# A two-layer graph network with top-p attention: fewer candidates in the second search, and one statistics step a slot later

## The chip, the cores and the metric

The kernel runs on one core of one Trainium2 chip. The metric is the time of one execution on the device in microseconds (us), lower is better; a kernel's time is the median of several runs. The core has five engines that work side by side[...]: TensorE (PE in the profile; its weight loads are shown apart as PEld), VectorE (DVE), ScalarE (ACT), GpSimd (POOL) and SyncE (SP), which only issues DMAs. Each engine carries out its own instructions in the order in which the program issues them.

## The reference

x is a table of 2708 nodes with 256 features, adj a sparse 2708 x 2708 adjacency (about 8 nonzeros a row and the diagonal). Layer 0 is

```
s = adj @ x
x = layernorm(x + relu(concat(x, s) @ weight + bias))
```

Layer 1 makes two steps on two streams, one over the row-normalised adjacency R (with the identity added), one over an attention A that is computed anew in each step:

```
for n in 0, 1:
    A  = top_p_attention(Xa)     # 2708 x 2708
    Xf = R @ Xf
    Xa = A @ Xa
    Z += Xf @ U1[n].T + Xa @ U2[n].T
h = layernorm(X + Z) * ln_g + ln_b
out = layernorm(x + h)
```

The attention takes the softmax of a bilinear form of the rows, keeps in each row the largest probabilities until those ahead of one sum to 0.9 (an element stays while the sum before it is under 0.9), sets the rest to zero and normalises the row again. Ties are cut in order of columns. So each row needs its own threshold.

## The kernel before, in words

**Blocks.** The 2708 rows are 22 blocks of 128 (the last, the edge, has 20). A block of attention is a tile `e` of 128 rows by 2708 (padded to 2720) columns. The kernel first does layer 0 (to about 290 us), then step 1 of layer 1 over the 22 blocks (to about 745 us), then step 2, where the change lies. The order of all instructions is written out by hand; nothing is planned by a scheduler.

**The fast path and the general path.** All of this is `fast_path`. It takes shortcuts in the search that need not hold for every input, and collects flags that tell whether they did. At the end the flags are summed, and if one is set, `general_path` computes layer 1 again with a plain search.

**The search of step 2.** Per block, ScalarE computes the exponentials and their sum z while it reads the logits (`exps2`, L844), and estimates from them a first level l0 (threshold z/l0). Two tries on ScalarE (`try_act`, L966 and L969: a Relu pass and a Sign pass over the block each) find the mass above a level; from it `next_level` makes the next level with the constants `STEPS`. `last_level` on VectorE picks the start: the last level if the count and mass rule with `FEW` accepts it, else the one before, else nothing. Then, all on VectorE:

- `below_level` (L1023): one pass over the block that keeps the elements below the start level in `low` and adds them up. It reads two tensors.
- `candidates` (L1030): the 8 largest of each of NS2 segments of SEG2 elements, by MAX8.
- `in_order` (L1039, L1042): the TOP2 largest of the candidates in order, by MAX8 and MATCH_REPLACE8 in turn, eight at a time.
- `threshold` (L1058 to L1078): a running sum over these, the element at which the mass reaches 0.9, and how many elements equal to it are kept in each of 4 windows of the row.
- `mark` (L1083), four times: writes the kept ties of one window into `w`.
- `mask` (L1088): one pass over the block that sets all below the threshold to zero and sums the rest. It reads two tensors too.

Afterwards TensorE transposes the masked block (`turn`, L527), ScalarE copies the transposes out (L530), and TensorE multiplies them with the values (`products`, L564).

**The loop of step 2.** One pass `per` of the loop works on four blocks at once: exponentials of block `per`+2, tries of block `per`+1, start level and candidates of block `per`, order, threshold, marks and mask of block `per`-1, product of block `per`-2. A pass has six slots g, one for each group of four transposes. In each slot TensorE's work is issued first, then ScalarE's, then one part of VectorE's (`next(vector)`, a generator in `vector_slots`), then what `later` holds, then `final_slot(g)`. The parts of VectorE are: slot 0 the first seven steps of the order in turn with the last-level arithmetic; 1 the below pass; 2 the rest of the order in turn with eight candidate segments, two at a time; 3 the threshold's steps in turn with the remaining segments, two at a time; 4 marks 0 and 1; 5 mark 2, the sum of z (L852, for block `per`+2), mark 3, two small operations, and the mask.

**The other stream.** Step 2's loop also carries both products with R. R is sparse, so each block m has a list of at most 896 columns, and `y_load` gathers the rows of the other operand: seven indirect DMAs (L719) of 128 rows of 1 KB, issued on GpSimd. Two buffers `yg` take turns; `r_load` issues block m+1's when block m starts. TensorE's units of it (`r_units`, L749, eight to a block) are spread over the slots: 144 over passes 2 to 9 for the first product, 176 over passes 11 to 21 for the second, which is 16 units or two blocks a pass.

**The end of a block.** When a block's two sums have met (`arrive`, L792), it is `ready`. `final_slot` brings it through two layernorms: slot 2 takes up to two ready blocks as `new`; slot 3 computes statistics of `new` and of `finals`, the blocks of the pass before (L1182, L1183: the first and the second layernorm); slot 5 the roots on ScalarE (L1218, L1219); slot 0 of the next pass one small product on VectorE (L1222), then for `finals` the last normalisation and for `new` the middle: a normalisation on ScalarE (L1192) into a `spares` tile and a multiplication and an addition on GpSimd (L1207, L1208), after which `new` become `finals`. These four GpSimd operations a pass stand in one queue with the gathers. Slot 1 stores what is done.

Of the kernel before, what the change touches and what calls it, by code (L numbers as in the profile page):

```python
# [21 lines left out]
CH = 512  # L22
SEG = 170
NS = 16
SEG2 = 136
NS2 = 20
TOP1 = 64
TOP2 = 48
WS = 4

GUESS = 2.76141059
STEPS = ((0.93339875, 14.44678062, 82.55022771), (0.98700001, 8.00991560, 128.06811957))
FEW = 20.0
TOP_S = 0.8999
TIE_EPS = 1.5e-5
KS = 7
# [14 lines left out]
def gnn_two_layer_kernel(ctx: ExitStack, tc: tile.TileContext, N, xT_d, x_d, adj_d, w0_d, b0_d,  # L53
# [29 lines left out]
    assert N % 2 == 0 and NB % 2 == 0 and N * 2.0 ** -15 < 0.09 and DC == 2 and DA == 64  # L83
    assert SEG * (NS - 1) + 8 <= N <= SEG * NS == SEG2 * NS2 and N >= SEG2 * (NS2 - 1) + 8
    assert NB == 3 * KS + 1 and CW == P and CAP % 8 == 0 and N < NB * P
# [63 lines left out]
def fast_path(ctx, tc, c, flags, fint, xT_d, x_d, w0_d, b0_d, w1_d, w2_d, w3_d, u1_d, u2_d, g_d, b_d):  # L149
# [297 lines left out]
    for m in range(NB):  # L447
# [35 lines left out]
        if m >= ML:  # L483
            i = m - ML
# [82 lines left out]
    def seg_max(dst, src, p, step, width):  # L567
        for i in range(NS):
            w = min(width, N - SEG * i) if step == SEG else width
            nc.vector.max(dst[:p, i * 8:(i + 1) * 8], src[:p, i * step:i * step + w])  # L570

    def put_in_order(dst, n, cand, p):

        spare = small.tile([P, NS2 * 8], FP, tag="spare", name="spare", bufs=1)[:, :cand.shape[1]]
        src = cand
# [11 lines left out]
    def extract1(t):  # L587
        p = rows(t)
        e = es[t % 4]
        cand = small.tile([P, NS2 * 8], FP, tag="cand", name="cand", bufs=2)[:, :NS * 8]  # L590
        seg_max(cand, e, p, SEG, SEG)
# [385 lines left out]
    def next_level(b, k):  # L977
        keep, slope, down = STEPS[k]
        nc.scalar.activation(b.kept, b.l[k], AF.Copy, scale=keep + TOP_P * slope, bias=-down)
        nc.scalar.activation((b.l1, b.l2)[k], b.u[k], AF.Identity, bias=b.kept, scale=-slope)  # L980
        if k:
            nc.scalar.activation(b.few, b.l1, AF.Copy, scale=TOP_P, bias=-FEW)

# [5 lines left out]
    def try_dve(b, k):  # L989
# [5 lines left out]
        if k == 0:  # L995
            keep, slope, down = STEPS[0]
            nc.vector.tensor_scalar(b.kept, b.l0, keep + TOP_P * slope, -down, op0=ALU.mult, op1=ALU.add)
# [20 lines left out]
    def below_level(b):  # L1018
# [5 lines left out]
                                       accum_out=bulk[:p, 2, t:t + 1])  # L1024
        b.cand = small.tile([P, NS2 * 8], FP, tag="cand", name="cand", bufs=2)

    def candidates(b):
        p = b.p
        for i in range(NS2):
            nc.vector.max(b.cand[:p, 8 * i:8 * i + 8], low[:p, SEG2 * i:SEG2 * (i + 1)])  # L1030
            yield

    def in_order(b):
        p = b.p
        b.srt = small.tile([P, TOP1 + 1], FP, tag="srt", name="srt", bufs=3)
        spare = small.tile([P, NS2 * 8], FP, tag="spare", name="spare", bufs=1)
        src = b.cand
        for i in range(0, TOP2, 8):
            nc.vector.max(b.srt[:p, i:i + 8], src[:p])  # L1039
            yield  # L1040
            if i + 8 < TOP2:
                nc.vector.match_replace(spare[:p], b.srt[:p, i:i + 8], src[:p], -3.0e38)  # L1042
# [3 lines left out]
    def threshold(b):  # L1046


        t, p = b.t, b.p
        s = b.srt[:p, :TOP2]  # L1050
        sc = small.tile([P, 3 + 2 * WS], FP, tag="sc", name="sc", bufs=3)
# [4 lines left out]
        x = sums  # L1056
        q_ = small.tile([P, TOP1], FP, tag="qs", name="qs", bufs=1)[:p, :TOP2]
        nc.vector.scalar_tensor_tensor(need, b.z, TOP_P - 1.0, below, op0=ALU.mult, op1=ALU.add)  # L1058
        nc.vector.tensor_tensor_scan(x[:p, 1:TOP2 + 1], s, s, 0.0, op0=ALU.add, op1=ALU.bypass)
        yield  # L1060
        nc.vector.scalar_tensor_tensor(q_, x[:p, 1:TOP2 + 1], need, s, op0=ALU.is_ge, op1=ALU.mult)
        yield
# [97 lines left out]
    new, finals, done = [], [], []  # L1160
# [56 lines left out]
    def roots(a, b):  # L1217
        nc.scalar.activation(sds[:, a:b], mvs[:, a:b, 1], AF.Ln, bias=c.eps, scale=1.0)  # L1218
        nc.scalar.activation(sds[:, a:b], sds[:, a:b], AF.Exp, scale=-0.5)  # L1219

    def over(a, b):
        nc.vector.scalar_tensor_tensor(nbs[:, a:b], mvs[:, a:b, 0], -1.0, sds[:, a:b], op0=ALU.mult, op1=ALU.mult)  # L1222

    def final_slot(i):


        if i == 2:
            while ready and len(new) < 2:
                new.append(Final(*ready.pop(0)))
                new[-1].load()  # L1230
        if i == 1:
            while done:
                done.pop().store()
        n = len(new) + len(finals)
        if i == 3:
            for k, f in enumerate(new + finals):
                f.stats(k)
        if i == 5 and n:
            roots(0, n)
        if i == 0 and n:  # L1240
            over(0, n)
            for f in finals:
                f.end()
            for f in new:
                f.middle()
            done[:] = finals
            finals[:] = new
            new.clear()
# [23 lines left out]
    for per in range(NB + 2):  # L1272
# [11 lines left out]
        for g in range(NG):  # L1284
# [30 lines left out]
            if g == 0:  # L1315
                final_slot(0)
                if t_mul:
                    t = t_mul - 1
                    base = za_load(t)
                    later[1].append(lambda t=t, base=base: arrive(t, base, accs.pop(t), ras.pop(t)[:rows(t)]))  # L1320
            for f in now:
                f()
            if g and (per < NB + 1 or g < NG - 1):
                final_slot(g)
# [407 lines left out]
```

## Time and profile before

| | us |
|---|---|
| median of 3 runs | 1303.6 (1302.28 to 1304.17) |
| the profiled execution, its own time | 1308.28 |
| its span (first to last instruction) | 1306.5 |
| PE busy | 1236.7 (95%) |
| DVE busy | 997.3 (76%) |
| ACT busy | 735.6 (56%) |
| POOL busy | 641.9 (49%) |

The profile is one execution, taken by the hardware profiler. Its page gives busy times by engine, the chain of work that ended last, and groups of instructions: line, engine, operation, what it writes and reads, how often, busy time and the mean duration of one, idle time of the engine before it and what ended that. The trace behind it answers for any stretch of time. A group's busy time counts overlapping instructions once, so busy over count is less than the mean duration. Times of a timeline are us from the span's start. A busy PE isn't PE at its peak, and an engine's gaps between instructions aren't counted as busy even where the engine could not have been faster.

The loop of step 2 runs from about 757 to 1290 us. The masks (L1088) start at 779.33, 810.42, 832.75, 856.54 and so on to 1282.64; from one to the next it takes between 20.7 and 25.2 us from the second on, and 15.5 us to the last.

### The profile page before, as it was taken

Reading aid. Unit: us, or ns where it says so; the run is one execution under the profiler, and the core shown is the slowest. Engines: PE = TensorE matmul, PEld = TensorE weight load, DVE = VectorE, ACT = ScalarE, POOL = GpSimd, SP = SyncE. Lnnn points to the kernel's source line nnn. Section 1 sums busy time; section 2 is a strip of 40 time slices with the busy share of each in tenths; the row PEclk is TensorE's granted clock in tenths of the full one; section 3 lists DMA queues with packets and bytes.
Section 4 is the critical chain, followed back from the end, with each engine's and each line's share of the span. In section 5 each row is a group of like instructions: output and inputs, shape, how many; then the busy total and the mean of one; then the engine's idle time right before and its main releaser. Section 6 shows DMA issues by size and latency. Waiting matters only on the chain.

```text
span 1306.5 us, 18895 instructions
## 1 busy us (share of the span) xinstructions
PE 1236.7 (95%) x5764; PEld 892.9 (68%) x5764; DVE 997.3 (76%) x3406; ACT 735.6 (56%) x1337; POOL 641.9 (49%) x594
## 2 busy tenths in 40 slices
PE   7999999979899999999999978999999999999975
PEld 5878778843477777777777556777765777766753
DVE  2455445884999997977771279989888999999996
ACT  1010110125456656655665488887888989989821
POOL 1000000002465442577666068878775778888850
PEclk9999999999999999999999888999999999999898
DMA  7455445423322220132324145565663645555551
GB/s 189 152 171 165 149 160 169 148 89 105 119 81 84 70 71 12 40 93 92 91 85 107 49 150 156 177 184 169 185 145 114 197 143 161 175 169 156 151 121 38
DMA packets 101704, 166.00 MB, mean 127 GB/s; under 512 B 17362, under 2 KB 74070, under 8 KB 101594
## 3 DMA queue, kind: packets, MB, share of 16 engines
q1 hardware_dynamic: 75308, 108.65, 26.0%
q0 software_dynamic: 20544, 51.17, 15.1%
q10 hardware_dynamic: 5742, 4.89, 1.4%
q8 instruction: 48, 0.79, 0.3%
q14 instruction: 62, 0.51, 0.1%
HBM read 130.74 MB, written 33.90 MB: 126 GB/s over the span
## 4 chain that ended last, share of the span: by engine, by line
PE 77%; DVE 10%; ACT 6%; DMA 3%; POOL 2%; issue 1%; SPq 0%; ACTq 0%; POOLq 0%; DVEq 0%
PE acc L564 26%; PE acc L257 16%; PE lg L507 9%; PE misc L749 9%; PE tr L527 7%; PE acc L651 2%; DVE e L1088 2%; DVE w L1083 2%; PE acc L462 2%; PE misc L426 2%; PE acc L672 2%; PE misc L699 2%; DMA xT<-in_xT 1%; POOL yg L719 1%; ACT e L844 1%
## 5 line engine op out<-in xcount | busy, mean ns | idle before, releaser
L530 ACT COPY wT<-tr 128x512 f32<-128x512 f32 (+2 forms) x258 | 132.0, 519 | 216.8 <-PE tr L527 215.8
L564 PE MATMUL acc<-x,wT 128*128 128x256 f32 (+1 forms) x924 | 230.5, 388 | 0.0
L564 PE MATMUL acc<-ya,wT 128*128 128x256 f32 (+1 forms) x924 | 228.1, 386 | 0.0
L719 POOL DMA_INDIRECT yg<-v_d,ix x154 | 196.6, 1277 | 59.8 <-issue 23.2
L719 POOL DMA_INDIRECT yg<-yf_d,ix x154 | 191.6, 1244 | 48.3 <-issue 23.1
L564 PEld LDWEIGHTS acc<-x,wT 128*128 128x128 f32 (+1 forms) x924 | 165.2, 189 | 71.0 <-issue 37.4
L257 PE MATMUL acc<-y,adj_t 128*128 128x257 f32 (+1 forms) x924 | 208.4, 381 | 0.0
L564 PEld LDWEIGHTS acc<-ya,wT 128*128 128x128 f32 (+1 forms) x924 | 170.6, 191 | 44.5 <-issue 24.0
L749 PE MATMUL misc<-yg,adj_t 128*128 128x256 f32 (+1 forms) x704 | 185.1, 396 | 14.0 <-DMA yg<-v_d,ix 6.6
L257 PEld LDWEIGHTS acc<-y,adj_t 128*128 128x128 f32 (+1 forms) x924 | 171.8, 189 | 32.7 <-issue 8.9
L367 POOL DMA_INDIRECT adj_t<-in_adj,ix x154 | 167.8, 1089 | 51.8 <-issue 44.1
L749 PEld LDWEIGHTS misc<-yg,adj_t 128*128 128x128 f32 (+1 forms) x704 | 124.2, 191 | 67.2 <-issue 21.5
L507 PE MATMUL lg<-k,q 64*128 64x512 f32 (+3 forms) x528 | 150.2, 596 | 14.0 <-ACT e L848 7.0
L527 PE MATMUL tr<-ident,e 128*128 128x128 f32 (+2 forms) x946 | 148.5, 276 | 7.5 <-DVE e L1088 6.3
L527 PEld LDWEIGHTS tr<-ident,e 128*128 128x128 f32 (+2 forms) x946 | 113.0, 140 | 52.1 <-issue 24.0
L334 POOL DMA_DIRECT2D part_d<-e x1 | 0.6, 573 | 290.3 <-DVE e L333 290.3
L966 ACT ACTIVATE e<-e,st 128x2708 f32<-128x2708 f32 (+1 forms) x43 | 113.5, 2640 | 0.1
L439 ACT COPY x1T<-tr 128x256 f32<-128x256 f32 (+1 forms) x22 | 8.0, 364 | 186.6 <-PE tr L438 186.6
L969 ACT ACTIVATE e<-e,st 128x2708 f32<-128x2708 f32 (+1 forms) x42 | 110.9, 2641 | 0.1
L570 DVE MAX8 cand<-e 128x8 f32<-128x170 f32 (+1 forms) x352 | 87.2, 317 | 26.6 <-ACT e L514 26.6
L1030 DVE MAX8 cand<-w 128x8 f32<-128x136 f32 (+1 forms) x440 | 105.9, 284 | 0.0
L1083 DVE MATCH_REPLACE8 w<-part,e 128x680 f32<-128x680 f32 (+1 forms) x88 | 74.3, 850 | 0.0
(238 smaller groups left out, 1732.3 us busy)
## 6 DMA issues: line engine op xcount, KB each, us to landing
adj_t<-in_adj SPq DMA_DIRECT2D x44, 704.0 KB
adj_t<-adjc_d SPq DMA_DIRECT2D x44, 448.0 KB
adjc_d<-adj_t SPq DMA_DIRECT2D x22, 256.0 KB
base<-za_d SPq DMA_DIRECT2D x40, 128.0 KB
adjc_d<-adj_t SPq DMA_DIRECT2D x22, 192.0 KB
xt<-in_x ACTq DMA_DIRECT2D x21, 128.0 KB
x_d<-x SPq DMA_DIRECT2D x21, 128.0 KB
x1b_d<-xb SPq DMA_DIRECT2D x21, 128.0 KB
```

The costliest lines, as they stand in the source:

```text
L257: nc.tensor.matmul(acc[:p, :n], lhsT=halves[k // KH][:kw, k % KH, :p], rhs=y[:kw, k, :n], start=k == 0, stop=stop and k == NB - 1)
L367: nc.gpsimd.indirect_dma_start(out=a[:CW, i, :], out_offset=None, in_=adj_rows, in_offset=bass.IndirectOffsetOnAxis(ap=ix[:CW, m, i:i + 1] ...
L507: nc.tensor.matmul(lg[:p, h, :b - a], lhsT=q[o, t * P:t * P + p], rhs=keys[s][o, i, :b - a], start=True, stop=True)
L527: nc.tensor.transpose(tr[:kw, k % 4, :p], e[:p, k * P:k * P + kw], ident[:p, :p])
L530: nc.scalar.copy(wT[:, :full, :p], tr[:, :full, :p])
L564: nc.tensor.matmul(acc[:p, :D], lhsT=wT[:kw, k % 4, :p], rhs=y[:kw, k, :], start=k == 0, stop=k == NB - 1)
L719: nc.gpsimd.indirect_dma_start(out=y[:CW, i, :], out_offset=None, in_=rows_d, in_offset=bass.IndirectOffsetOnAxis(ap=ix[:CW, m, i:i + 1], ...
L749: nc.tensor.matmul(acc[:p, :D], lhsT=a[:kw, k, :p], rhs=y[:kw, k, :], start=k == 0, stop=k == CC)
L966: nc.scalar.activation(scr[:b.p, :N], e, AF.Relu, bias=b.nz, scale=b.l[k], accum_out=b.relu)
L969: nc.scalar.activation(scr[:b.p, :N], e, AF.Sign, bias=b.nz, scale=b.l[k], accum_out=b.sign)
L1030: nc.vector.max(b.cand[:p, 8 * i:8 * i + 8], low[:p, SEG2 * i:SEG2 * (i + 1)])
L1083: nc.vector.match_replace(w[:b.p, W * i:W * (i + 1)], b.part[:b.p, i, :], e2(b.t)[:b.p, W * i:W * (i + 1)], 3.0e38)
```

## The change

Three things, all in step 2:

- The candidates come from 16 segments of 170 elements instead of 20 of 136: 16 MAX8 a block over 170 elements, and 128 candidates instead of 160. The four tie windows stay 680 elements wide, four segments each instead of five.
- 40 of the candidates are put in order instead of 48: five MAX8 and four MATCH_REPLACE8 over 128 elements instead of six and five over 160. The order stream has nine steps instead of eleven, so two are left for slot 2 instead of four; slot 3 is left with eight segments instead of twelve. The constants of the levels are others.
- In `final_slot`, the second statistics (of `finals`) are issued in slot 4, behind marks 0 and 1, instead of slot 3, behind the threshold. Those of `new` stay in slot 3.

```diff
-SEG2 = 136
-NS2 = 20
+SEG2 = 170
+NS2 = 16
 TOP1 = 64
-TOP2 = 48
+TOP2 = 40
 ...
-STEPS = ((0.93339875, 14.44678062, 82.55022771), (0.98700001, 8.00991560, 128.06811957))
-FEW = 20.0
+STEPS = ((0.97048, 13.37709, 72.87486), (1.01755, 9.09506, 145.60103))
+FEW = 17.8171
 ...
         if i == 3:
-            for k, f in enumerate(new + finals):
+            for k, f in enumerate(new):
                 f.stats(k)
+        if i == 4:
+            for k, f in enumerate(finals):
+                f.stats(len(new) + k)
         if i == 5 and n:
             roots(0, n)
```

## The prediction

> **What bounds the kernel now.** The page puts PE at 95% busy and at 77% of the chain that ended last, and DVE at 76%. But the change cuts DVE work in step 2 alone, so the shares over the span say little; I cut the span at the starts of the mask pass (L1088) and took the busy time of each engine in three such stretches (one pass each over a block):
>
> ```profile
> core 0: us, PE busy (x) PEld busy (x) DVE busy (x) ACT busy (x) POOL busy (x), PEclk, DMA share, GB/s
> 1023.51:1046.43 22.92, 22.92 (x112) 17.23 (x111) 22.05 (x82) 19.93 (x34) 18.34 (x16) 1.00 0.57 178
> ...
> 1118.46:1142.39 23.93, 23.64 (x113) 17.29 (x112) 23.69 (x87) 22.56 (x41) 20.05 (x17) 1.00 0.52 153
> ...
> 1167.58:1192.74 25.16, 23.61 (x112) 16.85 (x111) 23.72 (x86) 22.27 (x41) 20.89 (x19) 1.00 0.54 165
> ...
> ```
>
> The first is PE-bound (22.92 of 22.92 us): DVE time saved there is idle time. The second looks DVE-bound. In the third, which its two neighbours resemble (25.19 and 25.16 us), nobody is full: DVE 23.7, PE 23.6, POOL 20.9 of 25.16. Next, who waits for whom there. DVE's only wait from 1094 to 1268 us is the one that the change moves (us in total, times, longest):
>
> ```profile
> DVE bst L1182 <- POOL yg L1208: 6.5, 10, 0.9
> ```
>
> DVE waits for POOL, so POOL's timeline:
>
> ```profile
> 1186.45 0.73 POOL L1207 TENSOR_TENSOR yg<-yg,gb 128x256 f32<-128x256 f32 x1
> 1187.27 0.73 POOL L1208 TENSOR_TENSOR yg<-yg,x1b 128x256 f32<-128x256 f32 x1
> 1188.14 0.99 POOL L719 DMA_INDIRECT yg<-v_d,ix  x1
> 1189.43 0.95 POOL L719 DMA_INDIRECT yg<-v_d,ix  x1 [0.30 <-issue]
> 1190.69 0.95 POOL L719 DMA_INDIRECT yg<-v_d,ix  x1 [0.30 <-PE misc L749]
> 1191.94 0.95 POOL L719 DMA_INDIRECT yg<-v_d,ix  x1 [0.30 <-issue]
> 1193.19 3.41 POOL L719 DMA_INDIRECT yg<-v_d,ix  x1 [0.30 <-issue]
> ```
>
> POOL is full: a gather takes 0.95 us and 0.30 to the next, whatever the releaser, and from 1062.15 to 1262.76 us its timeline has no longer gap. Its 50% of the page counts these gaps as idle. The 3.41 us gather began 0.45 us into a DVE mask pass. Every one of the 30-odd gathers that began 0.11 to 1.2 us after the start of a 3.04 us two-input pass (L1023, L1088) ends 0.82 us after it; one already running when the pass starts keeps its 0.95, and so did two that began 0.01 and 0.03 us after the like pass of step 1 (L635). So a pass costs POOL 2.91 us less o, where o is the time from its start to the next gather's. The last link is DVE behind POOL's second L1208:
>
> ```profile
> 1188.03 0.43 DVE L1182 BATCH_NORM_STATS2 bst<-yg 128x6 f32<-128x256 f32 x1 [0.85 <-POOL yg L1208]
> ...
> 1190.63 0.08 DVE L1083 MATCH_VALUE_LOAD w<-part,e 128x8 f32 x1
> ...
> 1192.74 3.04 DVE L1088 SCALAR_TENSOR_TENSOR e<-w,st,e 128x2720 f32<-128x2720 f32 x1
> ```
>
> Statistics, four marks, mask: the pass starts 4.75 us after L1208 ends. A stretch on POOL is then 14 gathers x 1.2475 = 17.47, four final ops 3.02, mask 2.91-0.45 = 2.46, below pass (L1023, o = 0.66) 2.25: 25.2, measured 25.16. **POOL bounds this stage**; DVE's wait is how it shows.
>
> **What the Trainium skill says.** "SBUF — State Buffer", Who interferes with whom: a DVE op with two SBUF inputs and a GpSimd op exclude each other on a shared port, and the later one is blocked, not slowed. The trace agrees (0.95 to 3.4 us). "Perfetto Trace Analysis", DMA Instruction — SWDGE: a GpSimd DMA's end in the profile is its last descriptor, not its data; here loads into the gathers' buffer land 2.2 to 6.7 us after issue (median 3.8), so PE waits later than POOL's row ends. "TensorE: Matmul & The Clock Gate", What's actually happening: an idle window of about 3.4 us halves PE's clock. Here, after a PE load wait of 3.1 us, eight L564 entries took 3.41 instead of 1.73 us, and the stretch 1217.90:1242.54 had a clock of 0.86.
>
> **The change part by part**, for one block on DVE. Prices come from these groups (busy us, mean ns) and the timeline:
>
> ```profile
> L570 DVE MAX8 cand<-e 128x8 f32<-128x170 f32 (+1 forms) x352 | 87.2, 317 | 26.6 <-ACT e L514 26.6
> L1030 DVE MAX8 cand<-w 128x8 f32<-128x136 f32 (+1 forms) x440 | 105.9, 284 | 0.0
> L1039 DVE MAX8 srt<-spare 128x8 f32<-128x160 f32 (+1 forms) x110 | 34.9, 317 | 0.3
> L1042 DVE MATCH_REPLACE8 spare<-srt,spare 128x160 f32<-128x160 f32 (+1 forms) x88 | 27.0, 307 | 0.0
> ```
>
> Means include an overlapped tail, so I take starts. Candidates: 20 back to back took 4.11 us; 16 of 170 take 3.79 in step 1's chain: -0.3. Ordering: one MAX8 and one replace (with value load) go, 0.23+0.29 = -0.52 interleaved; the five and four left are 32 elements shorter, 0.032 us each by the same ops on 128 in step 1 (275 against 307 ns): -0.29. The equality test and count over 128: -0.07; five short ops over 40: -0.04. Against that, the limits' last steps lose their two covering candidate pairs: count to scan to part ran 0.35+0.26 us uncovered in the first block, 0.22+0.13 covered: +0.26. Sum **-0.95 us** a block. The new STEPS and FEW change data, not instructions.
>
> The move: `f.stats` for `finals` (two statistics, two aggregates; no DMA) goes behind marks 0 and 1 and the h add between (0.84+0.77+0.39). SP and POOL issue nothing in another order. Queued behind the waiting statistics are now marks 2 and 3, the z sums and mask; PE's transposes wait for the mask, ACT's roots for the statistics, not later than before. New start of the mask after L1208: 0.60 + (1192.74-1190.63) = 2.71 us instead of 4.75.
>
> What this is worth is read on POOL, which has the same 154 gathers in each half:
> - Mask pass. At +2.71 the third gather (it starts at +2.69) has just begun, so o = 1.23 and the cost is 1.68 instead of 2.45. Four blocks (stretches from 1142.39 on) are locked like this: -3.1. Three before them are not; from 2.29, 2.40 and 2.71 to the mean 2.28 of a random phase: -0.6. The last has no z sums, starts at +2.4, o = 0.29: +0.5.
> - Below pass. It follows the mask by 6.00 us, of which seven ordering steps shrink by 0.03 each: 0.23 sooner, so POOL resumes 0.23 sooner, in eight stretches: -1.8. In the first half (758 to 976 us, no longer gap on POOL either) seven such: -1.6. Cover: PE's 23.78 us cadence leaves 2.6 us of excess in 904:1003, so this is taken; were PE bound throughout, it would be 0.
> - End. POOL ends at 1262.76. The mask of block 20 comes 2.0 us sooner, but PE is busy until 1269.2 with units whose rows landed late, and waited 1.02 us for the mask until 1270.39: -1.15. The last block's uncovered ordering loses 0.79+0.29 and its threshold 0.1 on DVE; PE's products then end last, with 0.22 us of DVE wait gone: together **-1.4**.
> - Blocks 0 to 12 otherwise: nothing; PE, ACT (exps2) and POOL cover the 0.95 us. Without that cover it would be 12 us.
>
> Sum: -3.1-0.6+0.5-1.8-1.6-1.4 = **-8.0 us**. The profiled execution took 1308.28 us, 4.7 above the median shown; its span of 1306.5 becomes 1298.5, and the median 1303.6 becomes 1295.6. What is late next: PE's first units of a block, waiting for gathers.
>
> **Rivals.**
> 1. POOL's floor stays whole. The 0.02 us between the third gather's start and the mask is thin: if the lock takes hold earlier, that gather is held and costs 2.9. For: two nearly simultaneous starts is all I have. Then +0.4 instead of -0.77 on four blocks: -8.0+4.7 = -3.3, 1300.3.
> 2. All phase gains cancel and only the end counts: 1302.2. For: the first-half phases are accidents of PE's cadence.
> 3. DVE was the bound. Seven stretches (1094.24 to 1267.18, 172.9 us) fall to PE's 22.92: -12.5, with the end -13.9, 1289.7. For: DVE 23.7 of 23.9 at 1118. Against: POOL without a gap.
> 4. Slower: PE's clock. With the mask sooner and the gathers not, PE's idle time collects in one wait ahead of the first unit. It happened once (3.1 us); at clock 0.86 that stretch lost 0.14 x 24.6 = 3.4 us. From four such stretches on, 13.6-8.0 is slower than before by more than the bound: 1309. Against: idle PE falls from 2.5 (25.16-22.7) to about 1.3 us a stretch.
>
> That the change leaves the fast path: the reference's arithmetic on its inputs leaves at most 33 elements below the new start level to add (40 with the old), and none is hidden in a segment; 40 suffice. Under 1 in 100.
>
> **Chances.** Forecast 0.47, rivals 0.20, 0.15, 0.10, 0.08. A measurement of this kernel tells about 0.2%, 2.6 us. Faster: 0.46 + 0.15 (rival 1, mostly beyond 1301.0) + 0.03 + 0.10 = 0.74; within: 0.18; slower: 0.08. The forecast's own range is 1292 to 1299 (phases of three unlocked blocks +-0.4 each, first half +1.6 or -2). To hold 8 in 10 I reach to rivals 2 and 3: 1289 to 1303.
>
> **What would show it.** Right: POOL without gaps over 0.31 us from about 1060 to its last L1207; L1088 starting 2.7 us after L1208's end, gathers under its pass of 2.65 us; stretches of about 24.2 us; L1182 still waiting for L1208; PE's wait for L1088 smaller, for L719 larger. Wrong: POOL gaps of over 1 us or stretches of 22.9 (rival 3), gathers of 3.8 us (1), a clock of 0.86 in several stretches (4).

## The result, and the profile after

The changed kernel took 1295.79 us (median of 6 runs, 1291.2 to 1297.22) beside 1302.76 us for the kernel before: a ratio of 0.9937, 95% interval 0.9922 to 0.9952. Run once more later beside its two halves it was at 0.9952 (0.9937 to 0.9968). So the change saves 6 to 8 us (4 to 10 by the intervals); 8.0 had been forecast. The total is right, but its parts are not those of the sum.

The profiled execution took 1291.2 us (span 1289.4), the fastest of its kernel, while that of before (1308.28) was slower than all six of its kernel's timed runs. Of the 17.1 us between the two spans, 7.5 had arisen by the first gather of step 2's first half (757.70 against 750.20 us), ahead of every changed instruction. From here on stages are compared, not spans.

The groups of DVE that the change touches, of the kernel after (busy us, mean ns, idle before):

```profile
L1030 DVE MAX8 cand<-w 128x8 f32<-128x170 f32 (+1 forms) x352 | 94.2, 321 | 0.0
L1039 DVE MAX8 srt<-spare 128x8 f32<-128x128 f32 (+1 forms) x88 | 25.3, 287 | 0.3
L1042 DVE MATCH_REPLACE8 spare<-srt,spare 128x128 f32<-128x128 f32 (+1 forms) x66 | 18.2, 275 | 0.0
```

440 candidate operations became 352, and an ordering step costs 0.03 us less, as worked out. Stretches from one mask pass to the next, cut as before:

```profile
core 0: us, PE busy (x) PEld busy (x) DVE busy (x) ACT busy (x) POOL busy (x), PEclk, DMA share, GB/s
1012.24:1035.16 22.92, 22.92 (x112) 17.22 (x111) 21.00 (x75) 19.93 (x34) 18.34 (x16) 1.00 0.55 177
1106.95:1130.65 23.70, 23.63 (x113) 17.29 (x112) 23.39 (x79) 22.56 (x40) 19.82 (x17) 1.00 0.53 160
1130.65:1153.54 22.89, 22.57 (x108) 16.37 (x107) 21.97 (x79) 21.51 (x40) 18.92 (x17) 1.00 0.50 154
1153.54:1178.27 24.73, 23.20 (x111) 16.74 (x110) 22.27 (x80) 22.05 (x40) 20.45 (x19) 1.00 0.58 181
```

The PE-bound stretch of 22.92 us is the same to a hundredth, with DVE down from 22.05 to 21.00: there the saving became idle time. Stretches that took 25.16 us now take 22.9 to 24.8, and vary from one to the next. DVE's wait, which the move was to take away, has grown, from 6.5 us in 10 waits:

```profile
DVE bst L1182 <- POOL yg L1208: 10.4, 9, 2.7
```

It waits longer because it comes sooner; POOL is not quicker. POOL's timeline shows two outcomes, one at 1150 to 1157 us and one at 1199 to 1206 us (start, duration, operation):

```profile
1150.12 0.73 POOL L1208 TENSOR_TENSOR yg<-yg,x1b 128x256 f32<-128x256 f32 x1
1151.00 0.99 POOL L719 DMA_INDIRECT yg<-v_d,ix  x1
1152.30 0.94 POOL L719 DMA_INDIRECT yg<-v_d,ix  x1 [0.30 <-PE tr L527]
1153.54 0.96 POOL L719 DMA_INDIRECT yg<-v_d,ix  x1 [0.30 <-issue]
1154.81 2.59 POOL L719 DMA_INDIRECT yg<-v_d,ix  x1 [0.30 <-PE misc L749]
...
1198.98 0.72 POOL L1208 TENSOR_TENSOR yg<-yg,x1b 128x256 f32<-128x256 f32 x1
1199.86 0.99 POOL L719 DMA_INDIRECT yg<-v_d,ix  x1
1201.15 0.94 POOL L719 DMA_INDIRECT yg<-v_d,ix  x1 [0.30 <-PE misc L749]
1202.40 3.84 POOL L719 DMA_INDIRECT yg<-v_d,ix  x1 [0.30 <-issue]
```

and DVE's mask passes of these two places:

```profile
1153.54 3.04 DVE L1088 SCALAR_TENSOR_TENSOR e<-w,st,e 128x2720 f32<-128x2720 f32 x1
...
1202.38 3.03 DVE L1088 SCALAR_TENSOR_TENSOR e<-w,st,e 128x2720 f32<-128x2720 f32 x1
```

At 1153.54 the pass starts together with the third gather, which passes in 0.96 us; the fourth is held (2.59 us). At 1202.38 the third gather starts 0.02 us after the pass and is held for 3.84 us. POOL has no gap over 0.31 us in either half (the stretches from the first gather to the last of each product).

**One sum closes the account.** I add up, from POOL's timeline, what the gathers took beyond 0.95 us each ("held"), and compare with the time from the first final op (L1207) to the last gather's end. In us:

| kernel | that section | held in it (under mask / below passes) | section less held |
|---|---|---|---|
| before | 200.87 | 36.90 (19.38 / 17.58) | 163.97 |
| before, second trace | 201.08 | 37.06 (19.27 / 17.54) | 164.02 |
| move alone | 200.73 | 36.79 (19.26 / 17.60) | 163.94 |
| candidates alone | 199.24 | 35.45 (19.79 / 15.74) | 163.79 |
| both (after) | 199.08 | 35.27 (19.60 / 15.73) | 163.81 |
| both, second trace | 197.52 | 33.75 (18.09 / 15.74) | 163.77 |

Whatever DVE is given to do, the section is 163.9 us within 0.13, plus the time for which DVE's passes hold gathers. In the first half (first to last gather) the same subtraction gives 175.34 to 175.37 us in five of these traces (all but the second of before, which has waits of another kind there). So POOL never pauses in either half, and in the second the change acts only by where its passes fall between gathers. In the first half PE is full beside POOL for a time, as the bullet on it below shows.

### The profile page after: what moved, and what is told of

Same layout as the page of the kernel before. It is cut to its first block, busy times and chain, and to the rows that moved or that the text cites. A ratio compares the mean times of both kernels' runs of the same rounds, so it can differ in the third digit from the quotient of the medians.

```text
span 1289.4 us, 18741 instructions
## 1 busy us (share of the span) xinstructions
PE 1226.3 (95%) x5764; PEld 888.1 (69%) x5764; DVE 973.9 (76%) x3252; ACT 735.5 (57%) x1337; POOL 635.9 (49%) x594
## 4 chain that ended last, share of the span: by engine, by line
PE 79%; DVE 8%; ACT 7%; DMA 3%; POOL 2%; issue 2%; ACTq 0%; POOLq 0%; DVEq 0%
PE acc L564 27%; PE acc L257 16%; PE lg L507 9%; PE misc L749 8%; PE tr L527 7%; PE acc L651 2%; DMA yg<-v_d,ix 2%; PE acc L462 2%; PE misc L392 2%; PE misc L426 2%; PE acc L672 2%; ACT e L966 2%; PE misc L699 1%; DVE e L1088 1%; ACT e L844 1%
## 5 line engine op out<-in xcount | busy, mean ns | idle before, releaser
L719 POOL DMA_INDIRECT yg<-yf_d,ix x154 | 188.2, 1222 | 48.3 <-issue 22.5
L749 PE MATMUL misc<-yg,adj_t 128*128 128x256 f32 (+1 forms) x704 | 183.7, 394 | 14.9 <-DMA yg<-v_d,ix 5.9
L367 POOL DMA_INDIRECT adj_t<-in_adj,ix x154 | 171.3, 1112 | 52.0 <-issue 41.8
L749 PEld LDWEIGHTS misc<-yg,adj_t 128*128 128x128 f32 (+1 forms) x704 | 123.6, 189 | 67.6 <-issue 23.4
L527 PE MATMUL tr<-ident,e 128*128 128x128 f32 (+2 forms) x946 | 147.1, 274 | 3.1 <-DVE e L1088 2.0
L527 PEld LDWEIGHTS tr<-ident,e 128*128 128x128 f32 (+2 forms) x946 | 112.2, 138 | 44.8 <-issue 16.4
L334 POOL DMA_DIRECT2D part_d<-e x1 | 0.6, 573 | 285.6 <-DVE e L333 285.6
L1030 DVE MAX8 cand<-w 128x8 f32<-128x170 f32 (+1 forms) x352 | 94.2, 321 | 0.0
```

The costliest lines, as they stand in the source:

```text
L367: nc.gpsimd.indirect_dma_start(out=a[:CW, i, :], out_offset=None, in_=adj_rows, in_offset=bass.IndirectOffsetOnAxis(ap=ix[:CW, m, i:i + 1] ...
L527: nc.tensor.transpose(tr[:kw, k % 4, :p], e[:p, k * P:k * P + kw], ident[:p, :p])
L719: nc.gpsimd.indirect_dma_start(out=y[:CW, i, :], out_offset=None, in_=rows_d, in_offset=bass.IndirectOffsetOnAxis(ap=ix[:CW, m, i:i + 1], ...
L749: nc.tensor.matmul(acc[:p, :D], lhsT=a[:kw, k, :p], rhs=y[:kw, k, :], start=k == 0, stop=k == CC)
```

## Experiments

Two theories stand against each other: **POOL** (above) and **DVE** (its busy time sets the pace, so that 0.95 us a block is worth 0.95). The first four kernels ran on one chip, beside 1303.38 us for the kernel before. The other eight ran on two others, where the kernel before takes 1345.5 and 1347.2 us; the last heading tells what is seen of that. Those are compared by ratios within their group and by stretches.

**The two halves of the change.** The move alone, on the kernel before:

```diff
-            for k, f in enumerate(new + finals):
+            for k, f in enumerate(new):
                 f.stats(k)
+        if i == 4:
+            for k, f in enumerate(finals):
+                f.stats(len(new) + k)
```

> The kernel before with the second statistics (L1182 for finals) in slot 4 and nothing else. POOL theory (POOL bounds the stretches of step 2, a mask pass costs it 2.91 us less o, o the time to the next gather's start): the mask pass starts 2.7 us after L1208 instead of 4.75 in the stretches where DVE has to wait; what that gives is the luck of the phase, between 0 and -3 us in the 200 us from the first final op to the last gather; the first half (14 stretches before it) is unchanged within 1 us because finals do not exist there; the end gains 1.2 to 2.5 us because the mask of block 20 comes 2 us sooner. In all -1 to -5 us, most of it at the end. DVE theory (DVE's own time bounds): DVE's waits of 6.5 us go, so -5 to -7 us, all of it in the second half.

The candidates alone: the change with the lines above reversed.

> The change without its move: 16 segments of 170, 40 in order and the new constants, second statistics in slot 3 as before. POOL theory: only the distance from the mask pass to the below pass (6.00 us before, 5.77 after the whole change) counts, so -0.23 us for each of some 8 stretches of the second half (-1.8) and 7 to 14 of the first (-1.6 to -3.6), and -0.5 to -1.5 at the end from the last block's uncovered ordering: -4 to -7 us. POOL shows no gap over 0.31 us in both halves. DVE theory: -0.95 us for each of the 8 stretches, -7.6 in the second half alone, stretches there of at most 24.0 us instead of 24.8 to 25.2.

Both together, the changed kernel:

> The changed kernel once more, beside its two halves. POOL theory: the halves add up, -7 to -9 us against the kernel before, and its profile again shows POOL without a gap over 0.31 us, with the mask pass falling on either side of a gather's start in different stretches, so that some gathers are held for 3.8 us and some are not. DVE theory: the sum of the halves is larger than the whole, because the wait that the move removes is filled by the time that the candidates free.

Measured: move 1299.27 us, ratio 0.9974 (0.9957 to 0.9990); candidates 1299.05, 0.9968 (0.9957 to 0.9980); both 1297.54, 0.9952; before 1303.38. The halves add up within their intervals (-3.4 and -4.2 against -6.3 us). By stage the move gains nothing in the 200 us that it was aimed at (200.87 to 200.73, where the DVE theory wanted -5 to -7) and 2.06 us at the end, where the last gather is followed by block 20's mask after 5.41 instead of 7.47 us. The candidates gain 1.63 us in the second half, where the DVE theory wanted 7.6; stretches of 24.9 us stayed, against its at most 24.0. Both points speak for the POOL theory.

**Less work for POOL.** One of the two finals gets its two middle operations on DVE:

```diff
             spares.append(spares.pop(0))
+            if self.t_dve:
+                h, i, o = self.h, self.i, spares[-1]
+                nc.vector.scalar_tensor_tensor(o[:p], h[:p], mvs[:p, i, 0:1], c.gb[:p, 0, :],
+                                               op0=ALU.subtract, op1=ALU.mult)
+                nc.vector.scalar_tensor_tensor(o[:p], o[:p], sds[:p, i:i + 1], self.x1[:p],
+                                               op0=ALU.mult, op1=ALU.add)
+                self.h = o
+                return
             self.norm(spares[-1])
 ...
-            for f in new:
+            for k, f in enumerate(new):
+                f.t_dve = k == 0
                 f.middle()
```

> The changed kernel with the final's two middle operations of one of the two new blocks on DVE (two scalar_tensor_tensor of 128x256, as the tail does it) instead of one ACT and two POOL operations. POOL theory: POOL has 1.51 us less in each stretch of the second half, DVE 0.8 us more; stretches of 24.1 to 24.8 us fall to the 23.2 to 23.9 that DVE and PE need, so -5 to -9 us against the changed kernel, about 1288 us. DVE theory: DVE's 0.8 us more come on top in some 9 stretches, +5 to +7 us, about 1302 us. If PE's waits for gathered rows set the pace whatever POOL's total is: within 2 us of the changed kernel.

It took 1290.0 us (1287.25 to 1293.98), ratio 0.9900 (0.9880 to 0.9919), on the same chip 7.5 us below the changed kernel: more DVE work, less time. Two of its stretches:

```profile
1132.60:1155.75 23.15, 23.15 (x112) 17.16 (x111) 22.80 (x81) 21.86 (x39) 18.36 (x17) 1.00 0.58 182
1155.75:1178.89 23.14, 23.10 (x112) 17.03 (x111) 22.79 (x81) 21.78 (x39) 18.35 (x17) 1.00 0.57 182
```

Even stretches, a gap of 0.6 us on POOL in each from 1109 to 1202 us, and no wait of DVE between 1109 and 1247 us: POOL is out of the way; DVE (22.8 busy) and PE (23.1) are both full. The section to the last gather shrank by 10.6 us against the second trace of both; then the end gave part of it back (10.11 us from the last gather to block 20's mask, against 5.40), since DVE now trails.

The other way to relieve POOL is in the second half's loads of v_d. This kernel leaves out the gather of each block's seventh column group and puts a plain transfer in its place, so its result is not the reference's:

```diff
         for i in range(CC):
+            if s and i == CC - 1:
+                nc.sync.dma_start(out=y[:CW, i, :], in_=rows_d[:CW])
+                continue
             nc.gpsimd.indirect_dma_start(out=y[:CW, i, :], out_offset=None, in_=rows_d,
```

> The changed kernel with the seventh column group of each gather of the second half (the rows of v_d) read as one plain transfer of as many bytes on SP's queue, in place of an indirect one on POOL; the second product of R is wrong by that, and nothing else is left out. POOL theory: POOL has 1.25 us less in each of 22 blocks; the stretches of 24.1 to 24.8 us fall to the 22.9 to 23.5 of PE and DVE, -6 to -10 us from the first final op to the last gather, of which the end may give back up to 4 as PE then has its last units later than its rows: -4 to -9 us in all. DVE theory: within 1 us of the changed kernel.

Ratio 0.9866 (0.9840 to 0.9891). The section took 183.97 us, 13.6 to 15.1 less than the changed kernel: more than the 6 to 10 expected; and the end took 51.25 instead of 42.7 to 43.2, giving back 8 where up to 4 was expected. From block 11's mask to the end it is 247.63 against 254.20 and 253.16. Its stretches are PE's own (POOL has gaps of 0.8 us in them):

```profile
1152.59:1175.79 23.20, 23.18 (x111) 17.14 (x111) 22.46 (x80) 22.30 (x40) 18.73 (x17) 1.00 0.58 182
```

**More work for DVE.** With both finals on DVE:

```diff
-                f.t_dve = k == 0
+                f.t_dve = True
```

> As the run with one final's middle on DVE, but with both of them: POOL 1.5 us less again in each stretch, DVE 0.8 us more. With one, stretches were 23.14 us with PE 23.14 and DVE 22.80 busy and POOL had gaps; so if POOL is out of the way, DVE's 22.8 + 0.8 = 23.6 is the next bound: 0.3 to 0.6 us more in some 8 stretches, 2 to 5 us slower than with one, about 1293 us. If POOL still set the pace with one, this is faster than with one, by up to 5 us.

```profile
1153.89:1177.89 24.00, 23.20 (x113) 17.20 (x112) 23.62 (x83) 21.41 (x38) 17.39 (x14) 1.00 0.56 173
```

DVE's 23.6 us and 0.4 between its instructions are the stretch, seven times over, and POOL and PE have slack: DVE is the next bound. I had left the 0.4 out, so a stretch grew by 0.86 us instead of 0.3 to 0.6. From block 11's mask to the end it took 255.25 us against 250.16 with one, 5.1 us more, just past the upper end of what was expected; the ratio, on another chip than the version with one, was 0.9940 (0.9923 to 0.9958).

The other way to load DVE is four more candidate-like operations in the changed kernel:

```diff
         if b:
+            extra = small.tile([P, 8], FP, tag="extra", name="extra", bufs=1)
+            for i in range(4):
+                nc.vector.max(extra[:b.p], low[:b.p, SEG2 * i:SEG2 * (i + 1)])
             mark(b, 0)
             mark(b, 1)
```

> The changed kernel with four more MAX8 of 128x170 (1.29 us) on DVE ahead of the marks of every block from the second on, their result unused. POOL theory: DVE's time is covered by POOL and PE, the mask pass comes later only where DVE does not wait for L1208 anyway, and the distance from mask to below pass stays at 5.77; so nothing in the first half, phases only in the second (within 2 us either way), and at most 1.3 at the end: -1 to +3 us against the changed kernel. DVE theory: 1.29 us for each of 8 to 19 blocks, +10 to +24 us.

Neither theory had the number. The ratio was 0.9984 (0.9962 to 1.0007), and 258.20 us from block 11's mask to the end against 254.20 and 253.16: +4 to +5, beyond the POOL theory's +3 and far below +10.

```profile
1156.14:1180.68 24.54, 23.38 (x112) 17.06 (x111) 24.13 (x83) 22.31 (x40) 20.26 (x19) 1.00 0.57 172
```

In five stretches of 24.5 us DVE waited for nothing: 24.13 busy and 0.4 between instructions. POOL had no gap either. From block 12's mask to block 18's a stretch took 24.5 us in the mean, and 23.9 and 23.8 in the two traces of the changed kernel: of 1.29 us more work on DVE some 0.6 was covered, and then DVE reached POOL's time. The section to the last gather was even shorter (195.93 us, with 32.14 held, which leaves 163.79 again); what was lost came after it, 10.35 us instead of 5.4 to block 20's mask and 17.28 instead of 15.13 to the last. So DVE's slack is thinner than the POOL theory had it: about 0.6 us a block, and at the end none.

**Does the 0.95 us count once DVE is the bound?** Three kernels ask this: the edit with one final on DVE, made on the kernel before; the same on the candidates alone; and the same on the changed kernel again. "Old" and "new constants" stand for the whole first two points of the change, segments and ordering included.

> The kernel before, with old constants and the second statistics in slot 3, and one final's middle on DVE as in the run with one final's middle on DVE. Theory that the larger of POOL's stretch and DVE's busy time plus some 0.35 us sets the pace: DVE needs 22.8 + 0.95 (the candidates' saving is absent) + 0.35 = 24.1 us a stretch instead of 23.14, so from block 11's mask to the end about 258 us against 250.2 with the change's constants: here the 0.95 us that were covered in the changed kernel are paid in full, 8 times. If POOL alone set the pace in both: within 2 us of 250.2.

> The run with one final's middle on DVE, but with the second statistics back in slot 3, as before. There POOL's L1208 ends 4.2 us ahead of slot 3's statistics, so DVE would not wait in slot 3 either. POOL theory: the move is worth nothing once POOL is out of the way; 250 us (within 1.5) from block 11's mask to the end, and the same time over all. Theory that the move is a gain of its own: 3 to 6 us slower.

> The run with one final's middle on DVE once more, beside the two runs that undo a part of it: 250.2 us from block 11's mask to the end within 1 us, and 0.6 % below the changed kernel over all.

Ratios in this group: 1.0064 (1.0042 to 1.0086) with the old constants, 0.9966 (0.9948 to 0.9985) with the second statistics in slot 3, 0.9977 (0.9958 to 0.9997) for the whole. From block 11's mask to the end they took 271.0, 257.6 and 259.2 us, all of them off the forecasts because of stretches of up to 29.3 us with waits that this group's chip brings. What these leave undisturbed on the way to block 18: 24.06, 24.31 and 24.48 us with the old constants (24.1 forecast),

```profile
1159.03:1183.10 24.07, 24.01 (x116) 18.06 (x115) 23.79 (x89) 22.81 (x39) 19.22 (x17) 1.00 0.57 175
```

against 23.41, 23.65, 23.90 and 23.50 with the new. PE reads as busy for nearly all of the stretch shown, but DVE waited for nothing in it: its gaps between instructions add up to 0.28 us. The two stretches that follow are undisturbed in both as well, and there it is 23.55 and 23.62 us with the old against 23.50 and 22.96 with the new. By the ratios the new constants are worth 0.98% here (1.0064 to 0.9966), 13 us of 1347, where the same edit was worth 4.2 us with both finals on POOL. How much of the 13 these waits add is open. Where the same stretch is undisturbed in both, the old constants cost 1.07, 0.81, 0.05 and 0.66 us; so the saving is paid out in most stretches once DVE is full, but not in full in each. The move is worth nothing here: with and without it the undisturbed stretches are the same within 0.02 us (23.41, 23.90, 23.66, 23.51, 23.52, 22.97 without, 23.41, 23.90, 23.65, 23.50, 23.50, 22.96 with it). The version with one final on DVE was 0.6% below the changed kernel on the first chip; that this holds where such waits occur is not shown: in this group its ratio overlaps that of the next kernel, which is the changed one with a tiny copy.

**The edge.** A copy of 128x8 ahead of the mask pass, in the changed kernel:

```diff
         if b:
+            extra = small.tile([P, 8], FP, tag="extra", name="extra", bufs=1)
+            nc.vector.tensor_copy(extra[:b.p], ranks[:b.p])
             mask(b)
```

> The changed kernel with one tiny copy (128x8) on DVE between the z sums and the mask pass, some 0.07 us. In the changed kernel's two traces the pass starts 2.67 to 2.69 us after L1208's end where DVE waited for it, at the very start of the third gather, which is held or not by a hundredth of a microsecond. POOL theory: the pass now comes at about 2.75, no third gather is held, o is 1.17 and the cost 1.74 us in each such stretch but the last; from the start of block 11's mask to the end 252 to 254 us, against 254.2 and 253.2 in the two traces of the changed kernel; over the whole execution 0 to -2 us against it. Rival (a gather that has just begun can still be held): gathers under the pass of 3.75 to 3.85 us in those stretches, and +2 to +4 us.

It took 254.09 us from block 11's mask to the end, ratio 0.9961 (0.9930 to 0.9993): nothing gained. In two stretches the pass came 0.12 us after the third gather's start and the fourth took the hold, as wanted. In a third, block 18's, the pass came 0.05 us after that gather's start, and

```profile
1249.46 3.91 POOL L719 DMA_INDIRECT yg<-v_d,ix  x1 [0.30 <-issue]
```

a gather that had already started was held in full. This made me list, over all fourteen traces, every gather that starts between 0.10 us before and 0.08 us after the start of a two-input pass of some 3 us (L635, L1023, L1088): of 74, 69 took their usual time, whichever came first, and the five that were held are all under block 18's mask pass, in five kernels (at 0.05 ahead, and 0.02, 0.02, 0.05 and 0.05 after). All of the 21 that start 0.08 to 0.15 us after a pass are held. So the pass takes hold 0.08 us after its start in the profile, later than rival 1 of the prediction supposed, and the copy removed what was no cost. Block 18's pass is the one that follows z sums of 20 rows instead of 128 (the last block's); that this makes it take hold sooner is a guess.

**The kernel before again**, for a second trace:

> The kernel before once more, for a second trace of it. Expected by stage: about 217 us from the first gather of the first half to its last (216.9 with the move alone, which changes nothing there; 218.4 in the first trace of before), 200.9 from the first final op to the last gather, 7.5 from there to the mask of block 20, and 22.2 or 23.9 from the last mask to the end, the latter if the last block's 44 products (L550) again run at half clock. If the 1.7 us at the end came from the change, 23.9 is seen again; if from the chance of PE's clock, either can be.

The section and the end were 201.08 and 46.91 us (200.87 and 46.79 in the first trace), the 44 products (L550) again took 4.91 us, which either reading of the 1.7 us allows. The first half took 229.33, not 217, with the waits of that chip. Its ratio to the same kernel's other runs was 1.0018 (0.9998 to 1.0039).

## Why the prediction was right, and where it was not

| term of the sum, us | forecast | two traces of the changed kernel, against before |
|---|---|---|
| mask passes, second half | -3.2 | +0.2, -1.3 |
| below passes, second half | -1.8 | -1.85, -1.84 |
| first half | -1.6 | -3.6, -2.9 |
| end | -1.4 | -4.1, -3.6 |

- **POOL bounds the stage**: shown for the second half, by the six rows of the account and by the two kernels that relieve POOL (one at a price on DVE, the other with a plain transfer on SP's queue). Rival 3 (DVE the bound) falls; rival 2 (only the end counts) falls with the below passes. Rival 1 (the third gather is held) came true in one stretch of the first trace, block 18's, and in none of the second.
- **Candidates and order, -0.95 us of DVE a block, hidden**: right in the changed kernel. In the stretch of 22.92 us DVE lost 1.05. With one final on DVE it counts in most stretches, and it came through at the start of the loop (see the first half).
- **Below pass 0.23 us sooner**: right, term by term. From mask to below pass it is 5.77 us for 6.00, and the second half's held time under these passes fell by 1.85. In the first half it fell by 1.0 (23.37 to 22.35), not 1.6.
- **Mask pass: the step of the sum that failed.** -3.2 was forecast, +0.2 and -1.3 came. Stretch by stretch in the first trace, o before and after: 0.62 to 0.52, 0.51 to 0.25, 0.20 to 0.20 (the three that I had called unlocked: +0.4, where a random phase gave -0.6); 0.44 to 0.45 (I had counted it as locked at 1.23, but DVE reached the second statistics 2.1 us after POOL was done: 0 for -0.77); 0.46 to 1.27 (as forecast, 1.23); 0.45 to 0.67 (ACT's sum at L852 came 0.5 us late: -0.2); 0.45 to 0.02 (block 18, held: +0.4 for -0.77); 0.77 to 0.33 (the last, as forecast). The second trace had 1.27, 1.26 and 0.96 at blocks 16 to 18. So the mechanism held, the pass did come 2.67 to 2.69 us after L1208 where DVE waits, but I put too many stretches there. The chain of waits of before showed only where DVE waits for POOL; how much later it would come to the same place with the change, by the 2 us of marks put ahead, I did not check in each stretch. In "SBUF — State Buffer", Who interferes with whom, the Trainium skill has a DVE instruction with two SBUF inputs contend with a GpSimd instruction that reads SBUF, and calls the shared ports an exclusive lock. On the gathers' side the traces agree: in the first six no gather of step 2 took between 1.1 and 2.5 us. The other side is not seen: mask and below passes that began while a gather was running took 3.03 to 3.05 us, like the others, so here only the gather waits.
- **First half**: beyond the below passes, the mask passes there held 17.6 and 18.3 us instead of 20.2. No term stood for this. The move alone, which changes nothing there, has 19.0, so some 1.2 us of it is the luck of the phase, which rival 2 had spoken of; the remainder fits a shorter below distance shifting the following phases, which no run isolates. Nor is POOL the whole of it. In the move alone the gathers took 1.5 us less, but from the first of them to block 11's mask it gained only 0.3 us (288.7 to 288.4); with the new candidates that way took 285.0, 285.6 and 285.9. From block 1's mask to block 4's PE has no gap in four of these traces (0.2 us in the fifth), so what is to be gained there must come ahead of it, and it does: from block 0's mask to block 1's, where DVE waits only once, it took 31.09 and 31.14 us with the old candidates and 29.94 to 30.23 with the new. So DVE's saving came through at the start of the loop, where the forecast put nothing; its share in the first half's gain stays open.
- **End**: 2.06 us are the mask of block 20 (move) and 0.33 from mask to mask (candidates, 15.46 to 15.13). I had let PE's late units eat half of the first. In the first trace that lateness shrank too: PE's waits for rows (L749) ahead of block 20 fell from 2.57 and 0.59 us to 0.36, 0.77 and 0.96, and PE still waits 1.1 us for that mask, so the mask's whole gain came through. In the second trace PE waited 5.1 us for rows there and came too late to wait for the mask, and from the last mask to the end it took 0.5 us longer (22.68 us for 22.17). A further 1.64 us is PE's clock: the 44 products of the last block took 4.94 us in before, 3.30 in both traces after. A window inside them, before and after, shows the granted clock (third number from the end) at 0.50 and 1.00:

```profile
1289.00:1291.00 2.00, 2.00 (x24) 0.84 (x20) 1.46 (x10) 0.00 (x0) 0.00 (x0) 0.50 0.08 19
...
1273.50:1275.50 2.00, 2.00 (x32) 0.79 (x20) 1.51 (x10) 0.00 (x0) 0.00 (x0) 1.00 0.08 18
```

The version with one final on DVE showed 4.96 and 3.30 us in its two traces, with the same 0.60 us wait ahead. Of all fourteen traces five have the slow products (4.8 to 5.0 us), both of before among them, and nine the fast ones. So this isn't the change's doing with any certainty. "TensorE: Matmul & The Clock Gate", What's actually happening, in the Trainium skill says that the window over which PE's activity is judged runs freely; the two traces of one kernel agree with that.
- **Rival 4**: from block 2's mask to block 21's one stretch in each trace had a clock below 1.00 (0.93). It falls. PE's waits for the mask (L527), from 990 us to block 20's mask, fell from 5.3 to 1.1 and 0.9 us as forecast; those for gathered rows went from 6.6 to 5.9 and 8.1, which decides nothing.

The sum by stages is -9.5 and -9.8 us, the medians say -6 to -8. The profiled executions after were both the fastest of their group, and that of before was not; the difference is of the size of the phases' luck and the clock's 1.6 us. That the total came out near 8.0 is in part luck as well: the mask passes gave 1.9 to 3.4 us less than their term, and the first half and the end together gave 3.5 to 4.7 us more than theirs.

What stays open: why block 18's pass takes hold sooner, why the first half's mask passes fell better and how much of that half's gain is DVE's at the start of the loop, and the clock at the last products.

## What to carry to other kernels

Where GpSimd issues gathers back to back and DVE runs long two-input passes, count POOL's gaps between DMAs as busy and add up what each gather took over its normal duration: if the section less that sum stays constant, POOL is the bound. DVE's busy time as such then counts for nothing until its slack (here some 0.6 us a block) is used up; where its passes fall between the gathers does count. Take work off POOL first, even at a price on DVE: 0.8 us more a stretch there bought 7.5 us here. When an instruction that waits is moved behind others, work out for every stretch whether its engine still arrives before what it waits for; only there is the wait's time to be had.

## What the runs showed of the hardware that was not expected

- A two-input DVE pass holds indirect gathers that start from 0.08 us after its own start, not earlier, except the pass of block 18 (at the earliest 0.05 ahead, 3.91 us). Those held end 0.81 to 0.83 us after the pass. "SBUF — State Buffer", A bandwidth-pool intuition that's wrong (but worth ruling out), in the Trainium skill gives about 0.115 us after DVE's end for a GpSimd DMA behind a DVE copy; the gathers here need 0.82, most of their usual 0.95.
- On two of three chips the traces show idle time that ends with a releaser outside of this core's records, 31 to 66 us in 11 to 24 pieces; in the first six traces there is none. The waits of the kernel before on the second chip (us in total, times, longest):

```profile
ACT e L844 <- remote: 14.7, 4, 4.8
ACT wT L530 <- remote: 13.6, 7, 6.6
POOL yg L719 <- remote: 8.4, 5, 2.2
DVE e L1088 <- remote: 7.5, 1, 7.5
```

That is about the 42 to 44 us by which the kernel is slower there. What it is can't be told from one core's trace. None of them lies in the section from the first final op to the last gather, which took 201.08 us there and 200.87 in the first trace: what these waits leave alone is the same on both chips.
